# A graph network's edge constants loaded ahead of its branch, and its first edge attributes given space that is free at once

## The chip, the cores and the metric

The kernel runs on one core of one Trainium2 chip. The metric is device time in microseconds (us) of one execution. Before the change it is 2968.16 us, the median of three runs (2967.99 to 2969.02).

## What is computed

A graph of 6,250 nodes with 256 features each has 100,000 edges, sorted by destination, each with a source, a destination, 32 attributes and one of three types. Three layers run one after another on `x`, and a layer norm of the sum ends the work:

```python
ew = edge_attr @ edge_w + edge_b
for l in range(N_LAYERS):
    residual = x
    msg = jax.nn.relu(x[src] * ew)
    out = jnp.zeros((n, D), dtype=x.dtype)
    for i in range(NUM_REL):
        h = jax.ops.segment_sum(msg * rel_masks[i][:, None], dst, num_segments=n)
        h = h * inv_cnt[i][:, None]
        out = out + h @ weights[l, i]
    out = out + x @ roots[l] + biases[l]
    x = residual + jax.nn.relu(out)
...
return _layernorm(x + _L0_gnn_ref(x, ...), axis=-1)
```

## The kernel before

The outer function `tile_gnn_resnorm_kernel` first looks at the edge list: it loads sources, destinations and types (L1095 to L1100), works out on DVE (VectorE) whether the destinations are sorted and near enough to where they are expected, and writes a `flag` (L1156). All engines load that flag and branch on it (L1170, L1171). With these inputs the branch leads to `ordered_path`; `general_path` is for any other graph and doesn't run here.

Edges are handled in 391 **pairs** of two tiles of 128 edges, in an order that a planner makes (`order_of`). For each tile, POOL (GpSimd) issues one indirect DMA that gathers 128 rows of `x` into a tile `xs` (`gather_pair`, L1050 to L1055). So a layer has 782 gathers, and POOL's queue holds nothing but gathers once the branch is past. Four gathers (two pairs) share a buffer, and there are eight such buffers (`ROWS = 8`, L1047). The first six pairs (`FIRST = 6`, twelve gathers) go to spare room in `x_root` and are issued ahead of the branch (L1112 to L1116).

For two pairs together PE (TensorE) multiplies the edge attributes `at` by the edge weights `ew_sb` into PSUM (`make_ew`, L634). The bias of these products gets there in one of two ways. For the first four pairs a matmul of `full_ones` by `bias` puts it there (L630), where `bias` is the bias vector split into three bf16 parts. For all others ACT (ScalarE) copies `seed`, the bias on all partitions, to PSUM ahead of the matmul (L621). Then DVE multiplies the gathered rows by the result (`weigh`, L656), ACT applies the relu (L657), DVE makes one-hot matrices of the destinations (L669) and PE sums the messages by destination (`reduce`, L687 and L695). A buffer of `xs` is free for the next gathers when PE has read it. The order of all this is written out by hand in `layer`: iteration `it` gathers pair `it + 9`, makes the products of pair `it + 5`, weighs pair `it + 3` and reduces pair `it`. Interleaved with it, blocks of 128 nodes are finished (`node_mul`, `node_end`). SP (SyncE) issues the loads of `at`, eight pairs at a time in three buffers (`load_at`, L571), and the stores of finished nodes.

The change touches what lies between the branch and the first pairs. Behind the branch, before, ACT's queue issues the loads of `seed` (L486, two of 128 KB), `ew_sb` (L483, four of 32 KB, after DVE's clearing at L481) and `left` (L490, 128 KB), and only then clears two thirds of the sum table `acc` (L520). DVE splits `left` into its three parts (L496 to L503) in a pool `bias_s` of its own that is closed again at L504, so that its space is given to later tiles. `bias` is cast from the result (L503). `at` comes later, in the pool `edge` (L532).

Of the kernel before, what the change touches and what calls it, by code (L numbers as in the profile page):

```python
# [8 lines left out]
F32 = mybir.dt.float32  # L9
BF = mybir.dt.bfloat16  # L10
I32 = mybir.dt.int32
AF = mybir.ActivationFunctionType
ALU = mybir.AluOpType
# [429 lines left out]
def ordered_path(ctx, tc, x, attr_laid, A, weights, roots, biases, edge_w, edge_b, out, src, src_i, seg, place_i, consts, x_root,  # L443
# [6 lines left out]
    nc = tc.nc  # L450
    P = 128
    N, D = x.shape
# [13 lines left out]
    for u, (lo, hi) in enumerate(zip(least, most)):  # L466
# [3 lines left out]
            reach.append((lo % RING, hi % RING))  # L470
        else:
            reach.append((0, RING - 1))
    ident, ones, iota_w = consts

    dram = ctx.enter_context(tc.tile_pool(name="dram_o", bufs=1, space=DRAM))

    x_mid = [dram.tile([N + P, D], F32, name=f"x_mid{l}") for l in range(L - 1)]

    big = ctx.enter_context(tc.tile_pool(name="big", bufs=1))
    ew_sb = big.tile([P, 2, D], F32, name="ew_sb")  # L480
    nc.vector.memset(ew_sb, 0.0)  # L481
    for j in range(OCT):
        nc.scalar.dma_start(ew_sb[j * A:(j + 1) * A, j % 2, :], edge_w)  # L483
    seed = big.tile([P, 2, D], F32, name="seed")
    for i in range(2):
        nc.scalar.dma_start(seed[:, i, :], edge_b[None, :].to_broadcast([P, D]))  # L486
    bias = big.tile([PARTS, 2, D], BF, name="bias")
    with tc.tile_pool(name="bias_s", bufs=1) as bias_s:
        left = bias_s.tile([P, D], F32, name="left")
        nc.scalar.dma_start(left, edge_b[None, :].to_broadcast([P, D]))  # L490
        row = bias_s.tile([P, 1], F32, name="row")
        nc.vector.tensor_copy(row, node_i)
        is_row = bias_s.tile([P, PARTS], F32, name="is_row")
        part = bias_s.tile([P, D], BF, name="part")
        rows_of = bias_s.tile([P, D], F32, name="rows_of")
        nc.vector.memset(rows_of, 0.0)  # L496
        for k in range(PARTS):
            nc.vector.tensor_scalar(is_row[:, k:k + 1], row, float(k), None, op0=ALU.is_equal)
            nc.vector.tensor_copy(part, left)
            nc.vector.tensor_sub(left, left, part)  # L500
            nc.vector.scalar_tensor_tensor(rows_of, part, is_row[:, k:k + 1], rows_of, op0=ALU.mult, op1=ALU.add)
        for i in range(2):
            nc.vector.tensor_copy(bias[:, i, :], rows_of[:PARTS, :])  # L503

    x_all = big.tile([P, NT, D], F32, name="x_all")

# [4 lines left out]
    nc.vector.memset(zero, 0.0)  # L511
    eps = big.tile([P, 1], F32, name="eps")
    nc.vector.memset(eps, EPS)
    full_ones = big.tile([P, P], BF, name="full_ones")
    nc.vector.memset(full_ones, 1.0)
    for c in range(DC + 1):
        if c < DC // 2:
            nc.vector.memset(acc[:, c], 0.0)
# [5 lines left out]

    for rows_of in x_mid:
        nc.scalar.dma_start(rows_of[N - P:N, :], x_all[:, NT - 1, :])
    src_r = big.tile(list(src_i.shape), I32, name="src_r")
    src_e = big.tile([P, 2 * FIRST], I32, name="src_e")
    came = big.tile([P, 2 * FIRST, P], F32, name="came")
    came_i = came.bitcast(I32)  # L530

    edge = ctx.enter_context(tc.tile_pool(name="edge", bufs=2))  # L532
    rows = ctx.enter_context(tc.tile_pool(name="rows", bufs=ROWS))
# [394 lines left out]
OCT = 4  # L928
PARTS = 3
FIRST = 6  # L930
# [128 lines left out]
def kernel(ctx, tc, x, src, dst, edge_attr, edge_type, weights, roots, biases, edge_w,  # L1059
# [3 lines left out]
    nc = tc.nc  # L1063
    P = 128
    N, D = x.shape
# [9 lines left out]
    keep = ctx.enter_context(tc.tile_pool(name="keep", bufs=1))  # L1075
    ident = keep.tile([P, P], F32, name="ident_o")
    make_identity(nc, ident)
    ones = keep.tile([1, P], F32, name="ones_o")
    nc.vector.memset(ones, 1.0)
    iota_w = keep.tile([P, WK], F32, name="iota_w")  # L1080
    nc.gpsimd.iota(iota_w, pattern=[[1, WK]], base=0, channel_multiplier=0,
                   allow_small_or_imprecise_dtypes=True)
    node_i = keep.tile([P, 1], F32, name="node_i")
    nc.gpsimd.iota(node_i, pattern=[[0, 1]], base=0, channel_multiplier=1, allow_small_or_imprecise_dtypes=True)
    src_i = keep.tile([P, TC], I32, name="src_io")
# [2 lines left out]
    place_i = keep.tile([1, U], I32, name="place_i")  # L1088
    flag = keep.tile([1, 1], I32, name="flag")

    x_root = keep.tile([P, ROOTS, D], F32, name="x_root")

    with tc.tile_pool(name="look", bufs=1) as look, tc.tile_pool(name="look_p", bufs=2, space=PSUM) as look_p, \
# [4 lines left out]
        nc.scalar.dma_start(dst_raw, dst_laid)  # L1098
        typ_raw = look.tile([P, TC], I32, name="typ_raw")
        nc.sync.dma_start(typ_raw, type_laid)  # L1100

        limits = look.tile([1, 2, U], F32, name="limits")
        nc.gpsimd.iota(limits, pattern=[[2 * ASTRAY, 2], [2 * P, U]], base=-ASTRAY, channel_multiplier=0,
# [7 lines left out]
        first_rows = {}  # L1111
        for u in schedule(N, E, 1)[0][:FIRST]:  # L1112
            if u // 2 not in first_rows:
                j = 4 * len(first_rows)
# [27 lines left out]
        if last:  # L1142
# [25 lines left out]
                                       op0=ALU.mult, op1=ALU.add)  # L1168

    unordered = nc.values_load(flag[0:1, 0:1], min_val=0, max_val=1)  # L1170
    with tc.If(unordered == 0):  # L1171
        ordered_path(tc, x, attr_laid, edge_attr.shape[1], weights, roots, biases, edge_w, edge_b, out, src, src_i, seg, place_i,
                     (ident, ones, iota_w), x_root, first_rows, node_i)
    with tc.If(unordered > 0):
        general_path(tc, x, src, dst, edge_attr, edge_type, weights, roots, biases, edge_w, edge_b, out)

# [48 lines left out]
```

## Time and profile before

| what | value |
|---|---|
| median of three runs | 2968.16 us (2967.99 to 2969.02) |
| the profiled execution, own time | 2969.27 us |
| its span in the profile | 2967.0 us |
| mean granted clock of TensorE | 0.971 |
| PE busy | 2588.4 us, 87% |
| POOL busy | 2235.0 us, 75% |
| DVE busy | 1886.0 us, 64% |
| ACT busy | 1502.6 us, 51% |
| moved by DMA | 387.39 MB, mean 131 GB/s |

The profile has a timeline, which gives for each engine the start and length of its instructions and, in brackets, how long the engine was idle ahead of one and what ended that. It also has lists of who waited for whom, of groups of instructions by line, and of DMA issues. An engine's name with a q behind it (SPq, ACTq) is its queue, which issues DMAs. A busy share says little here: POOL is 75% busy, but the idle quarter is made of about two thousand gaps of 0.3 us between one gather and the next. Whether an engine sets the pace is seen from what ends its gaps.

### The profile page before, as it was taken

What the parts mean: (1) busy time and instruction counts of PE and PEld (TensorE: products, weight loads), DVE (VectorE), ACT (ScalarE), POOL (GpSimd) and SP (SyncE); (2) the same over time, 40 slices, a digit from 0 to 9 for tenths busy, and PEclk for the clock granted to TensorE, in tenths of its full rate; (3) what the DMA queues carried; (4) which work ended last, traced back from release to release, by engine and by line L of the source; (5) the groups of instructions that cost most, each with busy time, mean ns of one, the idle gap of its engine ahead of it and who ended that gap; (6) DMA issues with size and microseconds to landing.
All of it is one profiled execution on the core that took longest, in us unless ns stands there. A gap on an engine that the chain in (4) does not pass through costs nothing.

```text
span 2967.0 us, 43407 instructions
## 1 busy us (share of the span) xinstructions
PE 2588.4 (87%) x13712; PEld 1780.6 (60%) x13712; DVE 1886.0 (64%) x4910; ACT 1502.6 (51%) x1911; POOL 2235.0 (75%) x2355
## 2 busy tenths in 40 slices
PE   5999999999998788888988998778888988999886
PEld 2666677777765545555666666454555666666644
DVE  6656577777774545556666666445556677778754
ACT  4666656556565444454444444434444444444443
POOL 7777777777777777777777777777777777777776
PEclk9999999999999999999999999989999999999999
DMA  5444444444444444444444444444444444444443
GB/s 168 147 145 136 147 123 124 128 130 130 127 135 128 132 116 120 128 121 123 127 125 130 130 131 128 135 132 124 126 133 133 135 132 132 139 136 137 128 127 96
DMA packets 173705, 387.39 MB, mean 131 GB/s; under 512 B 43594, under 2 KB 79068, under 8 KB 173468
## 3 DMA queue, kind: packets, MB, share of 16 engines
q0 software_dynamic: 112608, 307.65, 36.1%
q1 hardware_dynamic: 53280, 68.50, 7.2%
q10 hardware_dynamic: 7580, 8.37, 0.9%
q8 instruction: 113, 1.85, 0.3%
q14 instruction: 124, 1.02, 0.1%
HBM read 364.89 MB, written 19.46 MB: 130 GB/s over the span
## 4 chain that ended last, share of the span: by engine, by line
PE 43%; DMA 17%; POOL 15%; issue 13%; DVE 7%; ACT 4%; DVEq 0%; POOLq 0%; ACTq 0%
POOL xs L1053 15%; DMA xs<-x_mid,src_r 14%; PE h_p L695 11%; PE ew_p L634 10%; PE h_p L687 9%; PE o_p L754 7%; DVE xs L656 5%; DMA xs<-in_x_dram,src_io 3%; PE r_p L736 3%; ACT xs L657 2%; ACT ew_p L621 2%; PE r_p L728 1%; PE h_p L707 1%; DVE x_root L739 1%; DVE acc L723 1%
## 5 line engine op out<-in xcount | busy, mean ns | idle before, releaser
L1053 POOL DMA_INDIRECT xs<-x_mid,src_r x1540 | 1465.5, 952 | 469.2 <-issue 367.8
L657 ACT ACTIVATE xs<-xs 128x1024 f32<-128x1024 f32 (+1 forms) x585 | 615.7, 1052 | 1315.7 <-DVE xs L656 1301.3
L656 DVE TENSOR_TENSOR xs<-ew_p,xs 128x1024 f32<-128x1024 f32 (+1 forms) x585 | 711.5, 1216 | 772.8 <-DMA xs<-x_mid,src_r 490.1
L1053 POOL DMA_INDIRECT xs<-in_x_dram,src_io x770 | 733.3, 952 | 235.1 <-issue 192.8
L695 PEld LDWEIGHTS h_p<-oh,xs 128*128 128x128 f32 x5160 | 663.5, 194 | 242.9 <-issue 114.5
L695 PE MATMUL h_p<-oh,xs 128*128 128x120 f32 x5160 | 725.7, 285 | 82.2 <-issue 36.6
L634 PE MATMUL ew_p<-ew_sb,at 64*128 64x512 f32 x2346 | 686.2, 661 | 101.0 <-ACT ew_p L621 96.9
L687 PE MATMUL h_p<-xs,oh 128*120 128x256 f32 x2088 | 575.4, 410 | 19.5 <-issue 5.7
L621 ACT ACTIVATE ew_p<-seed 128x1024 f32<-128x1024 f32 x582 | 588.8, 1012 | 0.0
L669 DVE TENSOR_SCALAR oh<-iota_w,seg_o 128x120 f32<-128x120 f32 x2346 | 512.6, 296 | 0.0
L754 PE MATMUL o_p<-w_sb,acc 128*128 128x256 f32 (+1 forms) x1728 | 440.1, 391 | 34.6 <-DVE x_root L785 31.2
L687 PEld LDWEIGHTS h_p<-xs,oh 128*120 128x120 f32 x2088 | 367.2, 193 | 161.9 <-issue 51.3
L723 DVE TENSOR_TENSOR acc<-h_p,acc 128x240 f32 (+1 forms) x732 | 323.7, 442 | 191.0 <-PE o_p L754 70.5
L754 PEld LDWEIGHTS o_p<-w_sb,acc 128*128 128x128 f32 (+1 forms) x1728 | 308.1, 190 | 158.6 <-DVE x_root L785 71.4
L634 PEld LDWEIGHTS ew_p<-ew_sb,at 64*128 64x128 f32 x2346 | 181.3, 189 | 230.6 <-ACT ew_p L621 124.5
L785 DVE SCALAR_TENSOR_TENSOR x_root<-o_p,inv,x_root 128x256 f32<-128x256 f32 (+1 forms) x432 | 207.0, 479 | 27.9 <-PE o_p L754 21.0
L736 PE MATMUL r_p<-r_sb,t_s 128*128 128x256 f32 x588 | 161.6, 398 | 33.0 <-ACT t_s L732 32.2
L771 ACT ACTIVATE acc<-zero_o 128x768 f32<-128x768 f32 (+1 forms) x150 | 140.2, 934 | 14.6 <-PE o_p L754 13.9
L673 ACT ACTIVATE oh_b<-oh 128x480 bf16<-128x480 f32 x196 | 116.2, 593 | 45.3 <-DVE oh L669 43.6
L736 PEld LDWEIGHTS r_p<-r_sb,t_s 128*128 128x128 f32 x588 | 103.5, 193 | 54.8 <-ACT t_s L732 43.1
L728 PEld LDWEIGHTS r_p<-ident_o,x_all 128*128 128x128 f32 x294 | 30.7, 143 | 167.3 <-DVE x_root L739 121.0
L728 PE MATMUL r_p<-ident_o,x_all 128*128 128x128 f32 x294 | 65.0, 303 | 69.2 <-DVE x_root L739 68.9
(110 smaller groups left out, 942.8 us busy)
## 6 DMA issues: line engine op xcount, KB each, us to landing
at<-in_attr_laid_dram SPq DMA_DIRECT2D x147, 256.0 KB
xs<-x_mid,src_r POOLq DMA_INDIRECT x1540, 2.8
xs<-in_x_dram,src_io POOLq DMA_INDIRECT x770, 2.8
x_mid<-x_all SPq DMA_DIRECT2D x96, 128.0 KB
x_all<-in_x_dram ACTq DMA_DIRECT2D x8, 768.0 KB
x<-in_x_dram SPq DMA_DIRECT2D x48, 128.0 KB
out_dram<-x_all SPq DMA_DIRECT2D x48, 128.0 KB
w_sb<-in_L_gnn_weights_dram SPq DMA_DIRECT2D x3, 768.0 KB
```

The costliest lines, as they stand in the source:

```text
L621: nc.scalar.activation(ew_ps[q][:, :n], seed[:, None, :, :].to_broadcast([P, n, 2, D]), AF.Copy)
L634: nc.tensor.matmul(ew_ps[q][:, k].rearrange("p i d -> p (i d)"), at[half, :], ew_sb[half].rearrange("p i d -> p (i d)"), start=False, stop ...
L656: nc.vector.tensor_mul(there, ew_ps[q][:, pairs.start:pairs.stop], there)
L657: nc.scalar.activation(there, there, AF.Relu)
L669: nc.vector.tensor_scalar(ohs[q][:, t, :], iota_w, seg[:, 4 * q + t:4 * q + t + 1], None, op0=ALU.is_equal)
L687: nc.tensor.matmul(h_p[:WK, :D], ohs[u // 2][:, t, :], xs[u // 2][:, u % 2, i, :], start=(i == 0 and first), stop=(i == 1 and closes(u)), ...
L695: nc.tensor.matmul(h_p[:, d * WK:(d + 1) * WK], xs[u // 2][:, u % 2, i, d * P:(d + 1) * P] if d < DC else full_ones, (ohs if d < DC else o ...
L723: nc.vector.tensor_tensor(there, h_ps[span][:, :CH * WK].rearrange("p (c r w) -> p c r w", c=CH, r=R), there, op=ALU.add)
L736: nc.tensor.matmul(rs[c][:, 1, :], t_ss[c][:, d, :], r_sb[:, d, :], start=(d == 0), stop=(d == DC - 1))
L754: nc.tensor.matmul(o_p[:n, j, :], acc[:, d, r, slot:slot + n], w_sb[:, r * DC + d, :], start=(d == 0), stop=(d == DC - 1))
L785: nc.vector.scalar_tensor_tensor(root, o_p[:n, j, :], inv[:n, c, r:r + 1], root, op0=ALU.mult, op1=ALU.add)
L1053: nc.gpsimd.indirect_dma_start(out=xs[:, u % 2, i, :], out_offset=None, in_=x_rows[:, :], in_offset=bass.IndirectOffsetOnAxis(ap=src_i[:, ...
```

## The change

Three things are done together. `ew_sb` and `seed` become tiles of the outermost pool `keep`; their clearing and their six loads are issued ahead of the branch, behind the load of the destinations. The bias is split out of `seed[:, 0, :]` instead of a third copy of it, so the load of `left` goes. The scratch of the split is put into `came`, a tile that lives to the end and isn't used until iteration 20, instead of into a pool that is closed; `came`, `src_r` and `src_e` are allocated first for that.

```diff
-    ident, ones, iota_w = consts
+    ident, ones, iota_w, ew_sb, seed = consts
...
-    ew_sb = big.tile([P, 2, D], F32, name="ew_sb")
-    nc.vector.memset(ew_sb, 0.0)
-    for j in range(OCT):
-        nc.scalar.dma_start(ew_sb[j * A:(j + 1) * A, j % 2, :], edge_w)
-    seed = big.tile([P, 2, D], F32, name="seed")
+    src_r = big.tile(list(src_i.shape), I32, name="src_r")
+    src_e = big.tile([P, 2 * FIRST], I32, name="src_e")
+    came = big.tile([P, 2 * FIRST, P], F32, name="came")
+    came_i = came.bitcast(I32)
+    full_ones = big.tile([P, P], BF, name="full_ones")
+    nc.vector.memset(full_ones, 1.0)
+    bias = big.tile([PARTS, 2, D], BF, name="bias")
+    scratch = came.rearrange("p t e -> p (t e)")
+    left, rows_of = scratch[:, :D], scratch[:, D:2 * D]
+    row, is_row = scratch[:, 2 * D:2 * D + 1], scratch[:, 2 * D + 1:2 * D + 1 + PARTS]
+    part = came.bitcast(BF).rearrange("p t e -> p (t e)")[:, 6 * D:7 * D]
+    nc.vector.tensor_copy(row, node_i)
+    nc.vector.memset(rows_of, 0.0)
+    for k in range(PARTS):
+        rest = seed[:, 0, :] if k == 0 else left
+        nc.vector.tensor_scalar(is_row[:, k:k + 1], row, float(k), None, op0=ALU.is_equal)
+        nc.vector.tensor_copy(part, rest)
+        nc.vector.tensor_sub(left, rest, part)
+        nc.vector.scalar_tensor_tensor(rows_of, part, is_row[:, k:k + 1], rows_of, op0=ALU.mult, op1=ALU.add)
     for i in range(2):
-        nc.scalar.dma_start(seed[:, i, :], edge_b[None, :].to_broadcast([P, D]))
-    bias = big.tile([PARTS, 2, D], BF, name="bias")
-    with tc.tile_pool(name="bias_s", bufs=1) as bias_s:
-        left = bias_s.tile([P, D], F32, name="left")
-        nc.scalar.dma_start(left, edge_b[None, :].to_broadcast([P, D]))
...
-        for i in range(2):
-            nc.vector.tensor_copy(bias[:, i, :], rows_of[:PARTS, :])
+        nc.vector.tensor_copy(bias[:, i, :], rows_of[:PARTS, :])
...
+    ew_sb = keep.tile([P, 2, D], F32, name="ew_sb")
+    seed = keep.tile([P, 2, D], F32, name="seed")
+    A = edge_attr.shape[1]
...
         typ_raw = look.tile([P, TC], I32, name="typ_raw")
         nc.sync.dma_start(typ_raw, type_laid)
+        nc.vector.memset(ew_sb, 0.0)
+        for i in range(2):
+            nc.scalar.dma_start(seed[:, i, :], edge_b[None, :].to_broadcast([P, D]))
+        for j in range(OCT):
+            nc.scalar.dma_start(ew_sb[j * A:(j + 1) * A, j % 2, :], edge_w)
```

ACT's instructions from the start of the program, before. A row has the line, the operation, the tile written and the tile read, the size, and the semaphores waited for (DMAHW and a number are those of the loads that SP and ACT issue):

```order
L1098 DMA dst_raw<-in_dst_laid_dram 128x782
L1170 TENSOR_LOAD flag [waits DVE_49]
L1171 COMPARE_AND_BRANCH
L486 DMA seed<-in_L_gnn_edge_b_dram 128x256 [waits DMAHW0_49,DVE_49,DMAHW3_49,PE_49,Pool_49]
L486 DMA seed<-in_L_gnn_edge_b_dram 128x256
L483 DMA ew_sb<-in_L_gnn_edge_w_dram 32x256 [waits DVE_49]
L483 DMA ew_sb<-in_L_gnn_edge_w_dram 32x256 [waits DMAHW1_49]
L483 DMA ew_sb<-in_L_gnn_edge_w_dram 32x256 [waits DMAHW2_49]
L483 DMA ew_sb<-in_L_gnn_edge_w_dram 32x256
L490 DMA left<-in_L_gnn_edge_b_dram 128x256 [waits DMAHW4_49]
L520 ACT_TABLE_LOAD
```

The same place in the changed kernel:

```order
L1093 DMA dst_raw<-in_dst_laid_dram 128x782
L1098 DMA seed<-in_L_gnn_edge_b_dram 128x256 x2
L1100 DMA ew_sb<-in_L_gnn_edge_w_dram 32x256 [waits DVE_49]
L1100 DMA ew_sb<-in_L_gnn_edge_w_dram 32x256
L1100 DMA ew_sb<-in_L_gnn_edge_w_dram 32x256 [waits DMAHW0_49]
L1100 DMA ew_sb<-in_L_gnn_edge_w_dram 32x256 [waits DMAHW1_49]
L1170 TENSOR_LOAD flag [waits DVE_49]
L1171 COMPARE_AND_BRANCH
```

Six loads have moved from behind the branch to between the load of `dst_raw` and the load of the flag, and that of `left` is gone.

SP's instructions behind the branch, before; `at` is loaded at L571:

```order
L1171 COMPARE_AND_BRANCH
L564 DMA r_sb<-in_L_gnn_roots_dram 128x2x256
L566 DMA b_sb<-in_L_gnn_biases_dram 128x256
L571 DMA at<-in_attr_laid_dram 128x512 [waits DMAHW5_49,DMAHW4_49,DVE_49]
L571 DMA at<-in_attr_laid_dram 128x512 [waits DMAHW6_49]
L571 DMA at<-in_attr_laid_dram 128x512 [waits DMAHW7_49]
```

And in the changed kernel, where these lines are L555, L557 and L562:

```order
L1171 COMPARE_AND_BRANCH
L555 DMA r_sb<-in_L_gnn_roots_dram 128x2x256 [waits DMAHW3_49]
L557 DMA b_sb<-in_L_gnn_biases_dram 128x256 [waits DMAHW4_49]
L562 DMA at<-in_attr_laid_dram 128x512 [waits DMAHW5_49]
L562 DMA at<-in_attr_laid_dram 128x512 [waits DMAHW6_49]
L562 DMA at<-in_attr_laid_dram 128x512 [waits DMAHW7_49]
```

The first load of `at` no longer waits for DVE; its order among SP's loads is the same, and `r_sb` and `b_sb` have each got a wait for a DMA semaphore.

More of the change, by code (lines that the diff above doesn't have):

```diff
@@ L479, in ordered_path @@
     big = ctx.enter_context(tc.tile_pool(name="big", bufs=1))
-    ew_sb = big.tile([P, 2, D], F32, name="ew_sb")
-    nc.vector.memset(ew_sb, 0.0)
-    for j in range(OCT):
-        nc.scalar.dma_start(ew_sb[j * A:(j + 1) * A, j % 2, :], edge_w)
-    seed = big.tile([P, 2, D], F32, name="seed")
-    for i in range(2):
-        nc.scalar.dma_start(seed[:, i, :], edge_b[None, :].to_broadcast([P, D]))
-    bias = big.tile([PARTS, 2, D], BF, name="bias")
-    with tc.tile_pool(name="bias_s", bufs=1) as bias_s:
-        left = bias_s.tile([P, D], F32, name="left")
-        nc.scalar.dma_start(left, edge_b[None, :].to_broadcast([P, D]))
[L491 to L501, printed above, removed]
-        for i in range(2):
-            nc.vector.tensor_copy(bias[:, i, :], rows_of[:PARTS, :])
@@ L513, in ordered_path @@
     nc.vector.memset(eps, EPS)
-    full_ones = big.tile([P, P], BF, name="full_ones")
-    nc.vector.memset(full_ones, 1.0)
     for c in range(DC + 1):
@@ L526, in ordered_path @@
         nc.scalar.dma_start(rows_of[N - P:N, :], x_all[:, NT - 1, :])
[L527 to L530, printed above, removed]
     edge = ctx.enter_context(tc.tile_pool(name="edge", bufs=2))
@@ L1172 @@
         ordered_path(tc, x, attr_laid, edge_attr.shape[1], weights, roots, biases, edge_w, edge_b, out, src, src_i, seg, place_i,
-                     (ident, ones, iota_w), x_root, first_rows, node_i)
+                     (ident, ones, iota_w, ew_sb, seed), x_root, first_rows, node_i)
     with tc.If(unordered > 0):
```

## The prediction

> **What bounds the kernel now.** I read the idle time first, not the busy time. The groups of instructions by line show who issues the most and what stands between:
>
> ```profile
> L1053 POOL DMA_INDIRECT xs<-x_mid,src_r x1540 | 1465.5, 952 | 469.2 <-issue 367.8
> L1053 POOL DMA_INDIRECT xs<-in_x_dram,src_io x770 | 733.3, 952 | 235.1 <-issue 192.8
> ...
> xs<-x_mid,src_e POOLq DMA_INDIRECT x24, 3.6
> ...
> x_root<-in_x_dram,src_f POOLq DMA_INDIRECT x12, 2.7
> ```
>
> Together these are 1540 + 770 + 24 + 12 = 2346 gathers. One takes 0.952 us, and the idle time ahead of one is (469.2 + 235.1) / 2310 = 0.305 us on the mean, so a gather comes every 1.257 us. The list of waits of POOL tells whether these gaps are waits for anybody. Its columns are the total, the number, and the longest one:
>
> ```profile
> POOL xs L1053 <- issue: 567.0, 1861, 0.3
> POOL xs L1053 <- ACT ew_p L621: 48.1, 158, 0.3
> POOL xs L1053 <- ACT t_s L732: 4.8, 14, 0.8
> ```
>
> The 0.3 us is there whether something released the gather or nothing did. So a gap of 0.3 us is the engine's own gap, and a real wait shows only in what exceeds it. One does in this list, with 0.8. The POOL timeline has its place, and the ends of the stream:
>
> ```profile
> 3.79 1.11 POOL L1053 DMA_INDIRECT x_root<-in_x_dram,src_f  x1 [1.46 <-DMA src_f<-in_src_laid_dram]
> ...
> 57.89 0.95 POOL L1053 DMA_INDIRECT xs<-in_x_dram,src_io  x1 [0.30 <-issue]
> 59.62 0.95 POOL L1053 DMA_INDIRECT xs<-in_x_dram,src_io  x1 [0.79 <-ACT t_s L732]
> ...
> 2951.01 0.95 POOL L1053 DMA_INDIRECT xs<-x_mid,src_r  x1 [0.30 <-issue]
> ```
>
> 2345 steps from 3.79 to 2951.01 are 2947.22 us, 1.2568 each: the stream runs without a break through all three layers. **The gathers of POOL set the time**: 3.79 us of start, 2947.2 us of stream, and 2967.0 - 2951.0 = 16.0 us from the last gather to the end. The page's other views point at PE, by its busy time and by its share of the chain of waits:
>
> ```profile
> PE 2588.4 (87%) x13712; PEld 1780.6 (60%) x13712; DVE 1886.0 (64%) x4910; ACT 1502.6 (51%) x1911; POOL 2235.0 (75%) x2355
> ...
> PE 43%; DMA 17%; POOL 15%; issue 13%; DVE 7%; ACT 4%; DVEq 0%; POOLq 0%; ACTq 0%
> ```
>
> I read that as work that runs beside the stream: the chain goes over PE wherever it can, and yet POOL waits for PE nowhere but in that one gap.
>
> **The change, part by part.** What it is about stands in the first 40 us of the timeline:
>
> ```profile
> 17.03 0.38 SPq L564 DMA_DIRECT2D r_sb<-in_L_gnn_roots_dram  x1
> 17.46 0.47 SPq L566 DMA_DIRECT2D b_sb<-in_L_gnn_biases_dram  x1
> 18.27 0.95 DVE L1167 SCALAR_TENSOR_TENSOR seg_o<-typ_t,off 128x782 f32<-128x782 f32 x1
> 19.38 0.82 ACTq L486 DMA_DIRECT2D seed<-in_L_gnn_edge_b_dram  x2
> 20.25 1.85 ACTq L483 DMA_DIRECT2D ew_sb<-in_L_gnn_edge_w_dram  x4
> 21.26 3.46 DVE L518 MEMSET acc<- 128x4080 f32 x1 [0.80 <-issue]
> 28.77 0.29 DVE L499 CAST part<-left 128x256 bf16<-128x256 f32 x1 [4.05 <-DMA left<-in_L_gnn_edge_b_dram]
> 32.46 0.48 DVE L503 CAST bias<-rows_of 3x256 bf16<-3x256 f32 x2
> 32.97 1.29 SPq L571 DMA_DIRECT2D at<-in_attr_laid_dram  x3
> 33.00 1.01 PE L630 MATMUL ew_p<-bias,full_ones 3*128 3x512 bf16 x2 [17.60 <-DVE bias L503]
> 37.19 2.17 PE L634 MATMUL ew_p<-ew_sb,at 64*128 64x512 f32 x4 [3.19 <-DMA at<-in_attr_laid_dram]
> ```
>
> *The first attributes.* SP is past the branch at 17.03 and done with `r_sb` and `b_sb` at about 17.9, but issues `at` only at 32.97, when the split has ended (32.94). That wait goes. The two new waits of `r_sb` and `b_sb` are for loads issued in the first microseconds and are over by then. `at` is issued at about 17.9 and, with the 4.2 us that it takes now (32.97 to 37.19), lands at about 22.1.
>
> *The split.* It waits for nothing any more, since `seed` has long landed. DVE is free of `seg` at 19.22. From the first cast to the end of `bias` it works 28.77 to 32.94, 4.2 us, and between its pieces stand now the clearing of `acc` (3.46) and some small clearings (about 1 us). So `bias` is ready at about 19.2 + 4.2 + 3.5 + 1 = 28 us instead of 32.94. ACT's clearing of `acc` is freed of the loads in the same way.
>
> *PE's start.* The first products come after the two bias matmuls (1.0 us), at about 29.1 instead of 37.19: PE starts 8.1 us earlier. **What is late next is the gathers**: the stream of POOL has the same rows in the same order as before, and its start at 3.79 hangs on the load of `src_f` alone. So nearly all of the 8.1 us is not on the path that sets the end, and I cost it at nothing, but for one piece.
>
> *The one wait of POOL.* The gather at 59.62 is the first that needs a buffer back: 32 gathers fill the eight buffers (19.08 to 57.89), and the 33rd needs the first one, which PE reads in these rows:
>
> ```profile
> 19.08 0.97 POOL L1053 DMA_INDIRECT xs<-in_x_dram,src_io  x1 [0.30 <-issue]
> ...
> 56.65 0.59 PE L687 MATMUL h_p<-xs,oh 128*120 128x256 f32 x2
> ...
> 58.69 0.17 PE L690 MATMUL h_p<-full_ones,oh_b 128*120 128x1 bf16 x1
> ```
>
> PE is done with it at 58.86, just too late: the gap is 0.79 instead of 0.305, which costs 0.48 us. With PE 8.1 us ahead the buffer is free at about 51, and the wait goes. **-0.48 us**, and it needs only 0.5 of the 8.1 us. If PE weren't ahead it would stay, 0.
>
> *What is added ahead of the branch.* DVE's clearing of `ew_sb` (0.48 us) moves to where DVE idles for POOL:
>
> ```profile
> 19.40 0.48 DVE L481 MEMSET ew_sb<- 128x512 f32 x1 [0.17 <-DVE seg_o L1167]
> ...
> 2.37 0.56 DVE L1109 TENSOR_SCALAR limits<-limits 1x782 f32<-1x782 f32 x1 [0.95 <-POOL limits L1103]
> ...
> 4.02 0.57 DVE L1118 CAST dst_t<-dst_raw 128x782 f32<-128x782 int32 x1
> ```
>
> It fits into that 0.95 us: nothing; without that cover it would push the flag by up to 0.48. The six loads stand on ACT's queue, where behind them only the load of the flag waits: nothing. But they move 256 + 128 = 384 KB beside the loads of `src_f`, `dst_raw`, `src_io` and `typ_raw`. If `dst_raw` lands later, so does the flag. How late may it be? These rows say it:
>
> ```profile
> 15.93 0.14 DVE L1156 TENSOR_SCALAR flag<-worst 1x1 int32<-1x1 f32 x1
> ...
> 17.83 0.95 POOL L1053 DMA_INDIRECT x_root<-in_x_dram,src_f  x1 [0.30 <-issue]
> ```
>
> SP needed 0.96 us from the flag (16.07) to its first issue (17.03). POOL still has gathers of the first twelve to run until 18.78, and its next begins at 19.08. With POOL's gap of 0.30, the flag may come 19.08 - 0.30 - 17.03 = 1.75 us later before POOL notices.
>
> `src_f` is another matter: each 0.1 us of it moves the whole stream by 0.1 us. It takes 2.77 us now:
>
> ```profile
> 0.74 0.39 SPq L1095 DMA_DIRECT2D src_f<-in_src_laid_dram  x1
> 0.74 0.40 ACTq L1098 DMA_DIRECT2D dst_raw<-in_dst_laid_dram  x1
> ...
> 0.74 2.77 DMA src_f<-in_src_laid_dram
> ```
>
> It is issued at 0.74, and the first added load after ACT is done with `dst_raw` at 1.14. No row shows this load with more beside it. From below I bound its delay by nothing (it could not get earlier, since all that is ahead of it stays), from above by `at`, which took 4.2 us in the busiest stretch of the transfers: 4.2 - 2.77 = 1.43. `at` would delay the flag no more either, and 1.43 is within the 1.75. I take 0, nearest to a load that is ahead of the others in its queue.
>
> The Trainium skill (DMA: Bandwidth & Descriptors, Issuing engines are not separate DMA queues) says that transfers started by ACT, SP and GpSimd end up on the same 16 DMA engines and interleave, so that a queue of its own protects `src_f` from nothing. By that rule the added loads cost something as soon as they are issued; no run here shows it yet, and the sum would be somewhere between the two ends above.
>
> *The other lengthened gathers.* Two in layer 0 stand out, beside long work of DVE:
>
> ```profile
> 90.61 0.97 DVE L578 SCALAR_TENSOR_TENSOR src_r<-src_io,src_r 128x782 int32<-128x782 int32 x1
> 91.02 1.38 POOL L1053 DMA_INDIRECT xs<-in_x_dram,src_io  x1 [0.30 <-issue]
> 100.05 1.35 DVE L765 TENSOR_TENSOR acc<-acc 128x1152 f32<-128x1152 f32 x1
> 100.25 1.96 POOL L1053 DMA_INDIRECT xs<-in_x_dram,src_io  x1 [0.30 <-issue]
> ```
>
> They are 0.43 and 1.01 us over 0.95. With PE and DVE earlier, these instructions meet the gathers at other points. From -1.44 (neither meets one) to +1.44 (as much again); I take 0. The moved clearings and the split cost the gathers nothing: the clearing of `acc` (21.26 to 24.72) had gathers of the usual length beside it.
>
> ```profile
> 22.85 0.94 POOL L1053 DMA_INDIRECT xs<-in_x_dram,src_io  x1 [0.30 <-issue]
> ```
>
> *Sum.* The profiled execution takes 2969.27 us, its span 2967.0; 2.27 lie around it. 2969.27 - 0.48 = 2968.79. That execution is 1.11 above the median of the runs, 2968.16; against the median, **2967.7 us**.
>
> **The rivals.**
>
> 1. *The gain at the front comes through.* Were PE the bound, as its 87% and its 43% of the chain suggest, the 8.1 us would come off: 2968.16 - 8.1 = 2960.1. Against it: POOL has one wait of 0.48 us and none later, so there is nothing in its stream to shorten. It would take a stream that PE holds up.
>
> 2. *Slower: the added loads delay `src_f`.* The mechanism is the shared transfers in the first 4 us, the place POOL's first gather at 3.79. It decides from 0.48 us of delay on, where it eats the gain. At its upper end, 2968.16 - 0.48 + 1.43 = 2969.1. To be slower by over 0.2% (5.9 us), `src_f` would have to take 2.77 + 5.9 + 0.48 = 9.2 us, far above the dearest load here. For it: the loads are really added there. Against it: they are issued later.
>
>    The Trainium skill's rule above speaks for this rival; the trace has no row against it, since before the change nothing but loads of the edge list stood there.
>
> 3. *The change doesn't do what it says*: `at` or the split still waits for something else behind the branch until about 33. Then PE starts as before, POOL's wait stays, and the time is 2968.2. Against it: the rows of SP and DVE show no such wait left.
>
> **How the numbers follow.** The forecast has 0.76, the first rival 0.05, the second 0.14, the third 0.05. About 0.2% is what a measurement of this kernel can tell from no change, 5.9 us, from 2962.2 to 2974.1. The forecast, the third rival and all but 0.03 of the second lie within: same 0.76 + 0.05 + 0.11 = 0.92; faster 0.05, the first rival; slower 0.03, the far end of the second. The range takes in the ends of the unknown costs: low 2967.7 - 1.44 = 2966.2, high 2967.7 + 1.43 + 1.44 = 2970.6. The runs themselves spread by 1.0 us, which I add in about equal parts: **2965.7 to 2971.1**. It leaves out the first rival and the far end of the second, 0.08.
>
> **What would show it.** In the profile of the changed kernel: the first `at` issued at about 18 and the first product of PE at about 29; no gap above 0.3 us ahead of the 33rd gather into `xs`; the first gather at about 3.8; the last gather about 0.5 us earlier than 2951.0, and 16 us behind it. The forecast is wrong if POOL's first gather moves, if POOL waits anywhere for the flag or a buffer, or if the stream's 1.257 us per gather changes; 0.001 us there is 2.3 us.

## The result: 4.2 us slower, by one gather

| | before | after |
|---|---|---|
| median | 2968.89 us (22 runs, 2967.38 to 2970.67) | 2973.13 us (22 runs, 2970.47 to 2974.57) |
| profiled execution, own time | 2969.27 us | 2973.04 us |
| its span | 2967.0 us | 2970.8 us |
| granted clock of TensorE | 0.971 | 0.973 |

The ratio is 1.0014, with a 95% interval of 1.0008 to 1.002. The forecast was 2967.7 us in a range that ended at 2971.1, so the time went to the other side and out of the range. The change is smaller than the 0.2% that the prediction called no change, but the interval lies wholly above 1.

The first fence is the row of that one wait in POOL's list of waits after the change, with the total, the number and the longest one. The second is the group of the gathers of layer 0, with busy time, mean ns of one, and idle time:

```profile
POOL xs L1044 <- ACT t_s L723: 4.9, 16, 0.3
```

```profile
L1044 POOL DMA_INDIRECT xs<-in_x_dram,src_io x770 | 737.1, 957 | 234.6 <-issue 191.6
```

The wait of 0.8 is gone from the list, and with it 0.5 us of idle time (235.1 before). But the gathers of layer 0 are busy for 3.8 us more (733.3 before), 5 ns each by the mean. That the mean hides a single one shows only in the timeline, whose columns are start, length, engine, line and instruction, and the idle time ahead. Rows of several engines are put in order of time:

```profile
3.74 1.16 POOL L1044 DMA_INDIRECT x_root<-in_x_dram,src_f  x1 [1.41 <-DMA src_f<-in_src_laid_dram]
...
17.97 1.38 SPq L562 DMA_DIRECT2D at<-in_attr_laid_dram  x3
...
21.05 0.50 DVE L496 CAST came<-came 128x256 bf16<-128x256 f32 x1
...
21.75 5.16 POOL L1044 DMA_INDIRECT xs<-in_x_dram,src_io  x1 [0.30 <-issue]
22.35 3.46 DVE L513 MEMSET acc<- 128x4080 f32 x1 [0.80 <-issue]
25.73 0.35 DVE L497 TENSOR_TENSOR came<-came 128x256 f32<-128x256 f32 x1
...
27.21 1.09 POOL L1044 DMA_INDIRECT xs<-in_x_dram,src_io  x1 [0.30 <-issue]
...
29.59 2.08 PE L625 MATMUL ew_p<-ew_sb,at 64*128 64x512 f32 x4
...
2954.34 0.95 POOL L1044 DMA_INDIRECT xs<-x_mid,src_r  x1 [0.30 <-DMA xs<-x_mid,src_r]
```

One gather, at 21.75, takes 5.16 us in place of 0.95. It isn't a gap ahead of the gather, so no list of waits has it. The last gather starts at 2954.34 in place of 2951.01, 3.33 later. The long gather is +4.21 of that (5.16 - 0.95), the other gathers of layer 0 are -0.4 (3.8 - 4.21), their idle time -0.5 and the first gather -0.05, together +3.3. From the start of the last gather to the end of the span it is 16.5 us in place of 16.0, and so the span is 3.8 us longer.

Beside the long gather, DVE clears `acc` (22.35), as it did before without harm. What is new is on both sides of the clearing: a CAST of the split directly ahead (21.05), and a subtraction of the split directly behind (25.73). The gather ends at 26.91, which is 0.83 us behind the end of that subtraction (26.08).

### The profile page after: what moved, and what is told of

Its sections match the earlier page's. It is cut to its first block, busy times and chain, and to the rows that moved or that the text cites. A ratio compares the mean times of both kernels' runs of the same rounds, so it can differ in the third digit from the quotient of the medians.

```text
span 2970.8 us, 43403 instructions
## 1 busy us (share of the span) xinstructions
PE 2586.2 (87%) x13712; PEld 1784.0 (60%) x13712; DVE 1883.7 (63%) x4910; ACT 1502.5 (51%) x1911; POOL 2238.9 (75%) x2355
## 4 chain that ended last, share of the span: by engine, by line
PE 45%; DMA 17%; POOL 13%; issue 12%; DVE 8%; ACT 5%; DVEq 1%; SPq 0%; POOLq 0%; ACTq 0%
DMA xs<-x_mid,src_r 13%; PE h_p L686 13%; POOL xs L1044 13%; PE ew_p L625 10%; PE o_p L745 9%; PE h_p L678 7%; DVE xs L647 5%; DMA xs<-in_x_dram,src_io 3%; PE r_p L727 3%; ACT xs L648 2%; ACT ew_p L612 2%; PE r_p L719 1%; PE h_p L698 1%; DVE acc L714 1%; DVE x_root L776 1%
## 5 line engine op out<-in xcount | busy, mean ns | idle before, releaser
L686 PEld LDWEIGHTS h_p<-oh,xs 128*128 128x128 f32 x5160 | 675.1, 197 | 239.4 <-issue 116.4
L686 PE MATMUL h_p<-oh,xs 128*128 128x120 f32 x5160 | 737.4, 289 | 80.3 <-issue 35.9
L678 PE MATMUL h_p<-xs,oh 128*120 128x256 f32 x2088 | 564.8, 404 | 21.6 <-DVE acc L714 6.9
L678 PEld LDWEIGHTS h_p<-xs,oh 128*120 128x120 f32 x2088 | 359.1, 189 | 159.9 <-issue 48.3
```

What stands on the lines that cost most here:

```text
L678: nc.tensor.matmul(h_p[:WK, :D], ohs[u // 2][:, t, :], xs[u // 2][:, u % 2, i, :], start=(i == 0 and first), stop=(i == 1 and closes(u)), ...
L686: nc.tensor.matmul(h_p[:, d * WK:(d + 1) * WK], xs[u // 2][:, u % 2, i, d * P:(d + 1) * P] if d < DC else full_ones, (ohs if d < DC else o ...
```

## The experiments

**First four: the CAST ahead, or the transfers?** The first theory was that the CAST ahead of the clearing makes the difference, and its rival that the transfers issued earlier (`at`, and behind them the first weights) do. These four ran on a chip on which the kernel before takes 3605.31 us (the four show a granted clock of 0.884 to 0.888), and their ratios to it (0.9985 to 1.0, intervals of 0.002 to 0.003 to either side) tell nothing at the size in question. The first 30 us of the traces, where an undisturbed gather takes its 0.95 us there too, do.

`late_at`: the changed kernel with the scratch of the split back in the pool that is closed, so that `at` and the weights behind it are late again.

```diff
+    with tc.tile_pool(name="bias_s", bufs=1) as bias_s:
+        left = bias_s.tile([P, D], F32, name="left")
...
-    scratch = came.rearrange("p t e -> p (t e)")
```

> The changed kernel, with the scratch of the split in a pool that is closed again, and came allocated late, as in the kernel before: so at waits for the end of the split again, at about 28 us, and w_sb behind it; the constants still come ahead of the branch and the split still takes seed. Nothing is left out. Theory 1 (shared access): VectorE's order is that of the changed kernel, cast and then clearing, so the long gather of about 5 us stays at about 22 us, and the time is 2972 to 2973. Theory 2 (transfers): 1.5 MB less are under way at 18 to 27 us, so no gather there is longer than 1.2 us, and the time is about 2968.5.

```profile
23.69 0.44 DVE L494 CAST part<-left 128x256 bf16<-128x256 f32 x1 [2.59 <-remote]
24.31 5.16 POOL L1047 DMA_INDIRECT xs<-in_x_dram,src_io  x1 [0.30 <-issue]
24.92 3.46 DVE L511 MEMSET acc<- 128x4080 f32 x1 [0.80 <-issue]
28.30 0.36 DVE L495 TENSOR_TENSOR left<-left,part 128x256 f32<-128x256 f32 x1
```

The long gather of 5.16 is there without the early `at`, which is issued only at 31.20 here. It moved with the clearing, from 21.75 to 24.31. These transfers are out.

`clear_first`: the changed kernel with the clearing of `acc` ahead of the whole split.

```diff
+    with tc.manual_schedule():
+        nc.vector.memset(zero, 0.0)
+        nc.vector.memset(eps, EPS)
+        nc.vector.memset(acc[:, 0], 0.0)
...
+        nc.vector.tensor_copy(row, node_i)
+        nc.vector.memset(rows_of, 0.0)
+        for k in range(PARTS):
```

> The changed kernel, with VectorE's clearing of acc (4080 columns) put ahead of the split instead of between its casts; nothing is left out. Theory 1 (shared access to SBUF: a cast from fp32 to bf16 on VectorE directly ahead of the long clearing keeps the next gather from starting until the clearing ends): ahead of the clearing stand only other clearings again, as in the kernel before, so no gather near 22 us is long (all 0.95 to 1.1 us), and the time is that of before less the one wait of 0.48: 2968.4. Theory 2 (transfers: at, w_sb, x_all, r_sb and b_sb, 2.7 MB issued between 17 and 20 us, fill the DMA engines, and the gather waits to hand over its rows): the loads are issued at the same times, so a gather of about 5 us stays near 22 us, and the time is about 2973.

The gathers beside the clearing started at 20.40, 21.65 and 22.91 and took 0.95 each: the order of DVE decides. Its time follows below, on another chip.

`before_plus_cast` and `before_plus_sub`: the kernel before, with a CAST or a subtraction directly ahead of the clearing.

```diff
+            with tc.manual_schedule():
+                nc.vector.tensor_copy(extra_b, extra_f)
                 nc.vector.memset(acc[:, c], 0.0)
```

> The kernel before, with one more VectorE cast of 256 columns from fp32 to bf16 (of a tile of zeros, into a tile that nothing reads) directly ahead of the clearing of acc. The transfers are those of before. Theory 1 (shared access): a gather that starts during the clearing now takes about 5 us instead of 0.95, and the time grows by 3.5 to 4.5 us to about 2972.9. Theory 2 (transfers): no long gather, and the time stays within 1 us of 2968.9.

> The kernel before, with one more VectorE subtraction of 256 columns, fp32 from fp32, both inputs in SBUF (its result is read by nothing) directly ahead of the clearing of acc; the control of the run with the cast. Theory 1 in its narrow form (it is the cast, which moves one input at more than one element a cycle): no long gather, 2968.9. Theory 1 in a wider form (any instruction that reads SBUF on both inputs ahead of the clearing does it): a gather of about 5 us and about 2972.9. Theory 2 (transfers): no long gather, 2968.9. A third theory, that it only depends on when a gather meets the beginning of the clearing and not on what stands ahead of it, would let this run and the run with the cast behave alike, since the clearing begins at about the same time in both.

```profile
22.15 0.50 DVE L522 CAST extra_b<-extra_f 128x256 bf16<-128x256 f32 x1 [1.16 <-DVE x_all L527]
22.84 0.95 POOL L1058 DMA_INDIRECT xs<-in_x_dram,src_io  x1 [0.30 <-issue]
23.45 3.46 DVE L523 MEMSET acc<- 128x4080 f32 x1 [0.80 <-issue]
24.09 0.94 POOL L1058 DMA_INDIRECT xs<-in_x_dram,src_io  x1 [0.30 <-issue]
```

With the CAST ahead of the clearing, as in the changed kernel, the gathers keep their length. `before_plus_sub` shows the same (22.93 and 24.18, 0.95 and 0.94). So my first theory fell, too. What was left is the instruction **behind** the clearing: in these two, as in the kernel before, there stands a CAST that waits for the load of `left` (28.77 there, 29.39 here); in the changed kernel and in `late_at` a subtraction that waits for nothing.

**The instruction behind.** The second theory: a DVE instruction that stands ready behind the running clearing keeps a gather from starting until it has ended. All runs from here on were on chips of the usual speed.

`sub_behind` and `cast_behind`: the kernel before, with its clearing of `acc` ahead of the split and one extra instruction behind it.

```diff
+    with tc.manual_schedule():
+        nc.vector.memset(extra_f, 0.0)
+        nc.vector.memset(acc[:, 0], 0.0)
+        nc.vector.tensor_sub(extra_g, extra_f, extra_f)
```

> The kernel before, with its clearing of acc moved ahead of the bias's split and one extra subtraction of two SBUF tiles (128x256, ready at once) directly behind the clearing. Theory (the instruction behind): a vector instruction with two SBUF inputs that stands ready behind the running clearing keeps a gather from starting until it has ended; one gather that starts during the clearing lasts until 0.82 us behind the end of the subtraction, some 3 to 5.2 us, no other gather near it is over 1.1, and the time is that of before plus 2.5 to 4.2 us (ratio 1.0008 to 1.0014). Rival (the clearing must follow a CAST as in the changed kernel): no long gather, ratio 1.000 within 0.0003.

> As sub_behind, but the extra instruction behind the clearing is a CAST with one SBUF input (128x256, ready at once). Theory (the instruction behind must have two SBUF inputs): no gather beside the clearing over 1.1 us, ratio 1.000 within 0.0003. Rival (any ready vector instruction with an input behind the clearing holds the gather): one gather of 3 to 5.2 us and ratio 1.0008 to 1.0014.

First the subtraction, then, in the second fence, the CAST (`nc.vector.tensor_copy(extra_g, extra_f)` with `extra_g` in bf16):

```profile
20.38 5.16 POOL L1057 DMA_INDIRECT xs<-in_x_dram,src_io  x1 [0.30 <-issue]
...
20.98 3.46 DVE L493 MEMSET acc<- 128x4080 f32 x1 [0.80 <-issue]
24.36 0.36 DVE L494 TENSOR_TENSOR extra_g<-extra_f 128x256 f32<-128x256 f32 x1
```

```profile
20.46 5.02 POOL L1057 DMA_INDIRECT xs<-in_x_dram,src_io  x1 [0.30 <-issue]
...
21.06 3.46 DVE L493 MEMSET acc<- 128x4080 f32 x1 [0.80 <-issue]
24.43 0.23 DVE L494 CAST extra_g<-extra_f 128x256 bf16<-128x256 f32 x1
```

One instruction of 0.36 us, ready behind the clearing, is enough for the long gather and for a loss of 3.1 us: 2972.8 us against 2969.68 of before beside it, ratio 1.0011 (1.0002 to 1.002). The gather ends 0.82 us behind the subtraction (25.54, 24.72). But the CAST does it as well: 5.02 us, 0.82 behind its end (25.48, 24.66), and 2973.15 us, ratio 1.0012 (1.0003 to 1.0021). So my narrowing to two inputs was wrong, and the rival of `cast_behind` is right: one input is enough. A CAST of the same kind and size stood behind the clearing in the kernel before, and barred nothing as long as it waited for `left`.

`memset_between`: the changed kernel, with a short clearing between the long one and the subtraction. DVE's order is written out by hand for that, and the clearing of `acc` falls into the first round of the split instead of the second.

```diff
             nc.vector.tensor_copy(part, rest)
+            if k == 0:
+                nc.vector.memset(acc[:, 0], 0.0)
+                nc.vector.memset(x_all[:, NT - 1, :], 0.0)
             nc.vector.tensor_sub(left, rest, part)
```

> The changed kernel, with the clearing of the last rows of x_all (128x256) put between the clearing of acc and the subtraction, in its order otherwise (CAST, clearing of acc, clearing of x_all, subtraction). Theory (the instruction directly behind the long clearing decides): the gather of 5.16 us is gone, at most one of 1.6 us is left beside the short clearing, and the time is 3.4 to 4.6 us below that of the changed kernel: 2968.4 to 2969.6 where before takes 2968.9 (ratio 0.9998 to 1.0002). Rival (the subtraction holds the gather from further back, or the CAST ahead of the clearing is the cause): a gather of about 5 us stays, ratio 1.0014.

```profile
21.00 3.46 DVE L511 MEMSET acc<- 128x4080 f32 x1 [0.80 <-issue]
...
21.64 0.95 POOL L1043 DMA_INDIRECT xs<-in_x_dram,src_io  x1 [0.30 <-issue]
...
24.46 0.27 DVE L512 MEMSET x_all<- 128x256 f32 x1
24.65 0.35 DVE L513 TENSOR_TENSOR came<-seed,came 128x256 f32<-128x256 f32 x1
```

Clearing and subtraction have the kind and size of those in the changed kernel, a CAST is ahead as there, and the long gather is gone. 2968.41 us, ratio 0.9996 (0.9987 to 1.0005): the 4.2 us are gone with it. That the order by hand isn't the reason is seen in `third_between` below, which has the same order without the short clearing, and a stall.

`clear_first_again` is `clear_first` once more.

> The changed kernel with the clearing of acc ahead of the whole split of the bias, so that a copy of 128x1 stands behind it: the kernel of clear_first once more, for its time. Theory: no gather over 1.1 us beside the clearing, and the time that the prediction gave the change without its long gather, 0.5 us under before (ratio 0.9997 to 1.0000). Rival (the added 4.2 us come from elsewhere in the change): ratio 1.0010 to 1.0014.

```profile
20.41 3.46 DVE L499 MEMSET acc<- 128x4080 f32 x1 [0.80 <-issue]
21.71 0.94 POOL L1041 DMA_INDIRECT xs<-in_x_dram,src_io  x1 [0.30 <-issue]
...
23.78 0.10 DVE L503 COPY came<-node_i 128x1 f32<-128x1 f32 x1
```

2968.86 us, ratio 0.9998 (0.9989 to 1.0007). Behind the clearing stands a ready instruction here too, a COPY, but of 128x1. So not each instruction with an input bars a gather. `memset_between` and this kernel have all of the change but the long gather, PE's early start included (29.41 and 29.10). Neither is faster than before by more than the runs can tell.

`third_between`: does the length of the clearing set the length of the stall?

```diff
+        nc.vector.memset(acc[:, 0, :R - 1], 0.0)
...
             nc.vector.tensor_copy(part, rest)
+            if k == 0:
+                nc.vector.memset(acc[:, 0, R - 1:], 0.0)
```

> The changed kernel with two thirds of the clearing of acc (128x2720) ahead of the first CAST, so that only 128x1360 is left between the CAST and the subtraction. Theory (a wide vector instruction with an input, ready behind a running clearing, keeps a gather that starts meanwhile from beginning until it has ended): the stall shrinks with the clearing, 1360 of 4080 columns are 1.4 of 4.26 us, so the longest gather there lasts 1.0 to 2.7 us in place of 5.16, ends 0.82 us behind the subtraction, and the time is 1.5 to 4.6 us below that of the changed kernel (ratio to before 0.9998 to 1.0009). Rival (the stall is a fixed price of this order of instructions): 5.16 us and ratio 1.0014.

```profile
23.21 1.19 DVE L512 MEMSET acc<- 128x1360 f32 x1 [0.23 <-issue]
...
24.18 1.31 POOL L1044 DMA_INDIRECT xs<-in_x_dram,src_io  x1 [0.30 <-issue]
...
24.31 0.36 DVE L513 TENSOR_TENSOR came<-seed,came 128x256 f32<-128x256 f32 x1
```

1.31 us in place of 5.16, ending again 0.82 behind the subtraction (25.49, 24.67). The stall isn't a fixed price: a gather that starts meanwhile waits for what is left of the clearing and the instruction behind it. 2969.64 us, ratio 0.9999 (0.999 to 1.0008).

**Which instructions.** Three kernels, one execution each, do the clearing six or eight times in a row, with another ready instruction behind each. Their edit is `sub_behind`'s, with these pairs repeated:

```diff
+        nc.vector.memset(acc[:, 0], 0.0)
+        nc.vector.tensor_copy(extra_g, extra_f)
+        nc.vector.memset(acc[:, 0], 0.0)
+        nc.vector.tensor_copy(extra_g[:, :1], extra_f[:, :1])
...
```

> The kernel of sub_behind with six clearings of acc in a row ahead of the split, and behind each another ready instruction: a COPY of 128x256 (float32 to float32), a COPY of 128x1, a multiplication by a constant of 128x256, a clearing of 128x256, a subtraction of 128x1, a clearing of 128x256. The clearings are done over again and the outputs of the extra instructions are not used. Theory (an instruction with an input and many elements bars the start): gathers of 3 to 5.2 us beside the 1st and 3rd clearing only, each ending 0.8 us behind the COPY and the multiplication, and gathers of 0.95 to 1.1 beside the others. Rival 1 (only a CAST or an instruction with two inputs does it, whatever its size): a long gather beside the 5th alone. Rival 2 (any instruction with an input does it, and it is another reason that spares clear_first): the 1st, 2nd, 3rd and 5th. The time says little here: each long gather is worth some 2.5 to 4.2 us.

> As kinds_wide with eight clearings and, behind them: a subtraction of 128x64, a bfloat16 clearing of 128x256, a subtraction of 128x16, a clearing, a CAST of 128x1, a clearing, a COPY of 128x64, a clearing. It looks for the width from which the instruction behind the clearing bars a gather, between the 128x1 COPY of clear_first (no long gather) and the 128x256 of cast_behind (5.02). Theory: 128x64 bars (a gather of 3 to 5.2 us beside the 1st and 7th), 128x1 does not, 128x16 is open. Rival (width does not matter, the kind does): the 1st, 3rd and 5th, not the 7th.

> As kinds_wide, with eight clearings and behind them, in turn with clearings of 128x256: a COPY of 128x128, a subtraction of 128x32, a COPY of 128x96, a subtraction of 128x48. In kinds_narrow a subtraction of 128x64 (2 x 64 = 128 elements read in a row) barred a gather and a COPY of 128x64 (64 read) did not. Theory A (the elements read count, from about 128 on): a gather of 3 to 5.2 us beside the 1st clearing (128 read), none beside the 3rd (64 read); the 5th and the 7th (96 read) go the same way as each other. Theory B (two inputs bar from a smaller width than one, by kind): the 7th may bar without the 5th, and the 1st need not. The clearings are done over again and the extra outputs are not used; the time says little.

The rows of the long gathers and of the instructions behind the clearings, in `kinds_wide`:

```profile
20.44 5.02 POOL L1068 DMA_INDIRECT xs<-in_x_dram,src_io  x1 [0.30 <-issue]
...
24.42 0.23 DVE L495 COPY extra_g<-extra_f 128x256 f32<-128x256 f32 x1
...
28.82 0.10 DVE L497 COPY extra_g<-extra_f 128x1 f32<-128x1 f32 x1
...
29.51 4.73 POOL L1068 DMA_INDIRECT xs<-in_x_dram,src_io  x1 [0.30 <-issue]
...
33.20 0.23 DVE L499 TENSOR_SCALAR extra_g<-extra_f 128x256 f32<-128x256 f32 x1
...
42.13 0.10 DVE L503 TENSOR_TENSOR extra_g<-extra_f 128x1 f32<-128x1 f32 x1
```

In `kinds_narrow`:

```profile
20.36 4.95 POOL L1072 DMA_INDIRECT xs<-in_x_dram,src_io  x1 [0.30 <-issue]
...
24.34 0.16 DVE L495 TENSOR_TENSOR extra_g<-extra_f 128x64 f32<-128x64 f32 x1
...
33.11 0.11 DVE L499 TENSOR_TENSOR extra_g<-extra_f 128x16 f32<-128x16 f32 x1
...
51.09 0.13 DVE L507 COPY extra_g<-extra_f 128x64 f32<-128x64 f32 x1
```

And in `kinds_edge`:

```profile
20.36 4.95 POOL L1071 DMA_INDIRECT xs<-in_x_dram,src_io  x1 [0.30 <-issue]
...
24.35 0.16 DVE L494 COPY extra_g<-extra_f 128x128 f32<-128x128 f32 x1
...
42.16 0.15 DVE L502 COPY extra_g<-extra_f 128x96 f32<-128x96 f32 x1
...
51.07 0.14 DVE L506 TENSOR_TENSOR extra_g<-extra_f 128x48 f32<-128x48 f32 x1
```

The four long gathers end 0.80 to 0.81 us behind the COPY of 256, the multiplication of 256, the subtraction of 64 and the COPY of 128 (for the first: 25.46 and 24.65). Beside all the other clearings of `acc` the gathers take 0.94 to 0.96.

| behind the clearing | elements read per partition | gather beside the clearing |
|---|---|---|
| CAST, COPY, multiplication of 128x256 | 256 | 5.02, 5.02, 4.73 |
| subtraction of 128x256 | 512 | 5.16 |
| COPY of 128x128, subtraction of 128x64 | 128 | 4.95, 4.95 |
| COPY of 128x96, subtraction of 128x48 | 96 | 0.94 to 0.96 |
| COPY of 128x64, subtraction of 128x32 | 64 | 0.94 to 0.96 |
| smaller ones, clearings | 0 to 32 | 0.94 to 0.96 |

So theory A of `kinds_edge` holds, and the 128x64 COPY of `kinds_narrow`, which I had expected to bar, goes with it: somewhere between 96 and 128 elements read by a ready instruction, with one input or two, the gather begins to be barred. This was seen with float32 inputs only, and for each row beside one or two clearings. Its length would draw the same line: the instructions with an input that barred take 0.16 us or more, the others 0.15 or less. No kernel here separates the two; a clearing of 0.27 us barred nothing, so length alone isn't it.

A short clearing counts, too. At the end of `kinds_narrow` one of 128x256 has a ready CAST of the split behind it, and the gather that starts meanwhile ends 0.81 us behind that CAST (56.78, 55.97):

```profile
55.55 0.27 DVE L509 MEMSET extra_g<- 128x256 f32 x1
55.59 1.19 POOL L1072 DMA_INDIRECT xs<-in_x_dram,src_io  x1 [0.30 <-issue]
55.74 0.23 DVE L521 CAST part<-left 128x256 bf16<-128x256 f32 x1
```

So `memset_between` is free of a stall also because no gather starts beside its short clearing: they start at 24.14 and 25.39.

Behind a subtraction it is different. In the changed kernel a gather starts while a subtraction runs and another ready instruction with two inputs stands behind it:

```profile
20.20 0.42 DVE L497 TENSOR_TENSOR came<-seed,came 128x256 f32<-128x256 f32 x1
20.35 1.09 POOL L1044 DMA_INDIRECT xs<-in_x_dram,src_io  x1 [0.30 <-issue]
20.54 0.48 DVE L498 SCALAR_TENSOR_TENSOR came<-came 128x256 f32<-128x256 bf16 x1
```

The gather ends 0.82 us behind the subtraction (21.44, 20.62), and not behind the second instruction (21.02). The gather at 27.21 does the same (28.30; the subtraction ends at 27.47, the instruction behind it at 27.87). So an instruction that stands behind counted where a clearing ran ahead of it, and not here.

The times of these three, 2983.59, 2993.48 and 2997.61, are more than their long gathers make. The clearings push the split, and with it PE's first product (55.10 in `kinds_wide`), so far back that the 33rd gather waits 8.7 us for its buffer (21.1 and 22.2 in the other two):

```profile
POOL xs L1068 <- ACT t_s L747: 10.8, 8, 8.7
```

That bears out the prediction's link between PE's start and POOL: a late PE reaches the stream through this one wait.

## Why the prediction was wrong, step by step

- *POOL's gathers set the time*: right. A gather 4.21 us longer at 21.75 is still there at 2954.34, less what the wait and some other gathers gave back. The time followed it.
- *The first attributes early*: right. `at` was issued at 17.97 (about 17.9 expected), and the first product came at 29.59 (29.1). These 7.6 us bought nothing but the wait of 0.48: right, too.
- *The added loads delay `src_f` by 0 to 1.43*: the value taken, 0, was right; the first gather came at 3.74 (3.79 before). That `src_f` is ahead of the others in its queue isn't shown to be the reason: the added loads went through ACT's queue, and `src_f` through SP's. The rule of the Trainium skill that I set beside it (DMA: Bandwidth & Descriptors, Issuing engines are not separate DMA queues) says that such loads interleave on the same 16 DMA engines. I took it for a cost as soon as they are issued; this trace shows none.
- *The failed step* is "The moved clearings and the split cost the gathers nothing: the clearing of `acc` (21.26 to 24.72) had gathers of the usual length beside it." The row was right, and the conclusion was not: I took the clearing by itself, and its harmlessness came from what stood behind it, a CAST waiting for a load. The change takes that load away. The split then no longer waits for anything, and a ready subtraction comes to stand behind the clearing. In place of 0 the term is +4.21 (5.16 - 0.95); with it the sum of the prediction, 2968.79, becomes 2973.0, and the profiled execution took 2973.04. That it fits so closely is luck in part: the other gathers gave 0.4 us back, and the end behind the last gather, taken as 16.0 us, took 0.5 more.
- *The bounds of the lengthened gathers*, -1.44 to +1.44, came from the two that the trace showed. Those two themselves stayed within them: the one of 1.38 us is there again (82.78, 1.40), and the one of 1.96 isn't, since the gather beside that addition of DVE (92.05) now starts 0.03 us ahead of it and takes 0.94. What the bounds left out is the clearing: `sub_behind`, `memset_between` and `third_between` show that what is left of it belongs to the price as well. A bound by it, 4.26 + 0.35 + 0.82 - 0.95 = 4.5 us, would have held the result.
- Those two rows had the mark in them, and I read only their size: the gather at 100.25 (before) ends at 102.21, 0.81 us behind the end of the DVE addition beside it (101.40), and the one at 91.02 ends 0.82 behind its own (91.58). It is the same ending as in each long gather above.

The Trainium skill (SBUF — State Buffer, Who interferes with whom) says that a DVE copy, cast or tensor_scalar in its two-port modes contends with GpSimd for ports that both use, that a DVE instruction with two inputs in SBUF does so with a GpSimd instruction that reads SBUF, that in the two-port modes whichever issues first has the ports for its whole instruction while the other is blocked, and that a DVE instruction with at most one input outside these modes doesn't contend. The kinds that barred a gather here are of those named, and the clearings by themselves barred none, so the traces agree so far. The same section tells of a probe in which `tensor_tensor` did not stall a DMA. That doesn't carry over to these gathers: a subtraction, which is one, stretched a gather to 5.16 us. By that section the clearing was safe, as I had it; that an instruction which stands behind a running clearing already blocks, I found in the runs and not in the page. That it is these ports, and not something else that the two engines share, was not measured here.

What stays open is why the number of elements, or the length, decides, and why a gather that starts while a clearing runs is barred by an instruction that, by its row, has not begun. A barring instruction behind anything else than a clearing was not tried on its own; the gathers at 20.35 and 27.21 are what is shown here on it, and the addition in the kernel before is one that bars while it runs.

## What to carry to other kernels

When a GpSimd stream of indirect DMAs sets the time, as here, the cost of a DVE instruction is not its length but what it bars, and with a long clearing ahead of it the clearing counts too. When a change takes a wait away, look at which instruction now stands ready behind the long ones: a row that was harmless before was so together with what followed it. Here a short clearing, or a copy of 128x1, between the two was enough to take the 4.2 us back, with no gather starting beside the short clearing.

## What the runs showed of the hardware that was not expected

- A ready DVE instruction that read 128 or more elements per partition (0.16 us or longer) kept an indirect DMA of GpSimd from getting done for what was left of the clearing ahead of it, and until 0.80 to 0.83 us behind its own end (5.16 us in place of 0.95). Up to 96 elements (0.15 us) it did not.
- A gather that comes first holds a CAST. In the changed kernel the CASTs of 128x256 at 19.70, 21.05 and 26.68 begin in the second half of a gather, take 0.47, 0.50 and 0.34 us in place of 0.23 (`cast_behind`) to 0.29 (the kernel before), and end 0.11 to 0.12 us behind the gather (20.05, 21.44 and 26.91).
- The row of a long clearing seems to start late. For 4080, 2720 and 1360 columns the idle time ahead and the length are 0.80 + 3.46, 0.52 + 2.33 and 0.23 + 1.19 us, so the sum goes with the columns, 1.04 to 1.05 ns each. The gather at 21.75 started in the 0.80 us that the profile calls idle and was barred already.
- On one chip the kernel before took 3605.31 us, where the traces of the four kernels show a granted clock of 0.884 to 0.888. Most of the idle time that the stream of gathers gained there has no releaser in the profile, as in this row of POOL's list of waits in `before_plus_sub`: 1047.1 us in place of 567.0, with a gap of up to 4.8 us where the other chips have 0.3. Waits for ACT and PE grew as well. The cause is open:

```profile
POOL xs L1058 <- issue: 1047.1, 2080, 4.8
```
